# One set of rows per tile in the third stage: layer 2's scale and layer 3's statistics go back to rows together

## The chip, the cores and the metric

The kernel runs on one core of one Trainium2 chip. The metric is the device time of one execution in microseconds (us). The engines are named as in the profile: PE (TensorE; PEld is its loading of weights), DVE (VectorE), ACT (ScalarE), POOL (GpSimd) and SP (SyncE, which issues most transfers).

## The reference

The input x has 8192 samples of 8 channels of 16 x 16. Four layers follow each other, each of the form x = x + layer(gn(x)), where gn normalises each sample in 4 groups of 2 channels (mean and variance over 512 values). Layer 0 applies a tensor-train matrix and a bias. Layer 1 is a 3 x 3 convolution with batch normalisation and relu. Layers 2 and 3, the ones that matter here, are:

```python
# layer 2: quantised 3 x 3 convolution; sx comes from the largest |gn(x)| of all samples
sx = MAX_Q / jnp.max(jnp.abs(x));  sw = MAX_Q / jnp.max(jnp.abs(weight))
out_i32 = conv(_quantize(x, sx), _quantize(weight, sw))
out = out_i32 / (sx * sw) + bias
# layer 3: 3 x 3 convolution with edge padding, weights = sign times a mean of |w|
out = conv(pad(x, mode='edge'), binarize(weight)) + bias
```

In both, x inside the layer is gn(x); outside it is the running x.

## The kernel before, in words

The samples are cut into 64 tiles of 128 samples. A tile is [128 partitions, 2048 columns]: a partition is one channel and row of the image (c, h), a column is a sample and a w. A convolution is then three matmuls with banded 128 x 128 weights, one for each shift in w; 512 columns make one PSUM bank, two banks are half a tile.

There are three stages. The first does layer 0 and layer 1's convolution. The second adds layer 1 (its batch statistics are known by then), takes layer 2's statistics of every sample into `gnst`, subtracts the mean and finds the overall maximum. Then `sx` is formed, and the third stage does the rest of layer 2 and layer 3 for each tile. It takes tiles in `order`: first the 13 that stayed in SBUF, then the others, which are loaded from HBM four tiles ahead.

Statistics of a sample are made as columns with one sample per partition ([128, 4] for four groups), but are needed along the columns of a tile, the same for the 32 partitions of a group. The way back has two steps. `to_rows` multiplies each column by a mask into a diagonal tile `diag` on DVE (one product for each set of four columns) and transposes it in 32 x 32 blocks into `rows`. A matmul with a constant 0/1 selection matrix (`sel0`, `sel1`, `corr`) then spreads one set of columns over all partitions, into PSUM: `r2` (in `ps_a`) is layer 2's scale, `r3` (`ps_r`) layer 3's, `o3` (`ps_o`) layer 3's offset.

The operations of one tile i in the third stage, with engine and names as the profile shows them:

- `rows2` (DVE: diag_d, rows_d) and `spread2` (PE: ps_a<-rows_d): scale of layer 2.
- `scale2` "v" (DVE, two halves: v<-x,ps_a, to int8), `round2` "q" (ACT: q<-v, to bf16).
- `layer2` "c2h1", "c2h0" (PE: pq<-q,band, six matmuls for each half of the tile).
- `bias2` (ACT) adds the bias to half 0 of x; `first2` "stz" (DVE) adds half 0 of the product, pq x inv; `second2` "z1" (ACT: bs<-pq) writes half 1 into z3 and `add2` "add1" (POOL) adds it to x.
- `square3` "sq" (ACT), `sums3` "sums" (PE: s<-x,wsum and s<-sq,wsum, with 32 output columns each, four side by side in the array).
- `stats3` "small" (DVE: a reduction, a transposition into `st3`, then in `stats_small` a copy, a product and the variance into mv), `pow3` (POOL: mv to the power -1/2).
- `rows3` (DVE: mr = mean x scale, three diagonal products diag_e, transposition rows_e), `spread3` (PE: ps_r, ps_o<-rows_e), `offset3` "c" (ACT).
- `scale3` "t" (DVE, two halves), `high3` "hi" (ACT: rounds t, then the edge columns), `low3` "lo" (POOL: t - hi), `add3` "corr" (POOL: x + c), `edges3` "edl" (ACT: the edge columns of lo).
- `layer3` "c3h0a", "c3h0b", "c3h1a", "c3h1b" (PE: pf<-hi,sign and pf<-lo,sign; for each half of the tile six matmuls with hi and six with lo); `finish` "out0", "out1" (DVE: x<-pf,scale,x); after the second of them SP writes the tile out.

Tiles overlap as in a modulo schedule. Each operation has a time in `PHASE`; all operations of all tiles are sorted by PERIOD x i + PHASE (last lines of `tile_net`) and are issued in that order, through `InOrder`, which keeps each engine's program order. The times are sort keys alone: what runs when is decided on the chip by each engine's queue and the semaphores. Since `InOrder.__getattr__` issues nearly all operations, the profile gives L43 for them, and one goes by the names of tiles. PSUM is full: two slots of two banks for pq and pf together (`ps_c`), and a bank each for ps_a, ps_r, ps_o and s.

```python
todo = [(op, i) for _, op, i in sorted((PERIOD * i + at, op, i) for op, at in PHASE.items() for i in range(NT))]
for op, i in todo:
    if op == "rows2" and AHEAD <= i + 4 < NT:
        load3(i + 4)
    OPS[op](i)
```

Of the kernel before, what the change touches and what calls it, by code (L numbers as in the profile page):

```python
# [22 lines left out]
G = 4  # L23
# [9 lines left out]
class InOrder:  # L33
# [5 lines left out]
    def __getattr__(self, name):  # L39
        op = getattr(self.engine, name)  # L40

        def call(*args, **kwargs):
# [2 lines left out]

PERIOD = 11.539
PHASE = {"rows2": 0, "spread2": 0.01, "v": 5.1, "q": 10.2, "bias": 10.4, "c2h1": 11.6, "z1": 13.1, "c2h0": 16.1, "add1": 17.1,
         "stz": 23.1, "sq": 24, "sums": 31.8, "small": 34.7, "pow": 37.3, "rows3": 42.7, "spread3": 45.3, "t": 46.3,  # L50
         "hi": 49.9, "c": 51.2, "lo": 51.9, "corr": 58.8, "edl": 60.3, "c3h0a": 60.4, "c3h0b": 61.3, "out0": 66.8,
         "c3h1a": 69.3, "c3h1b": 69.4, "out1": 69.41}

PACK0 = [("c0", R * C), ("c1", R * H), ("core2", 2 * R * W), ("bias0", W)]
# [5 lines left out]
def tile_net(ctx: ExitStack, tc: tile.TileContext, xb, xt_in, pack0, pack1, pack2, out):  # L62
# [33 lines left out]
    T2 = [dict() for _ in range(NT)]  # L96

    LATE = 5 if NT >= KEEP + STAY + 3 else 0

    def load2(i, what="yx"):  # L100
        for k in what:
# [45 lines left out]
    def late_constants(late):  # L147
# [101 lines left out]
        quarter = L["quarter"] = blocks(32, 1.0, "quarter")  # L249
        gpad = L["gpad"] = const.tile([P, NQ, 32], F32, name="gpad")  # L250
        dve.memset(gpad, 0.0)
        dve.tensor_copy(gpad[:, :, 0:G], quarter.unsqueeze(1).to_broadcast([P, NQ, G]))
        for k, name in enumerate(("sel0", "sel1", "corr")):

            t = L[name] = const.tile([P, CH], F32, name=name)
            dve.tensor_copy(t.rearrange("p (g n) -> p g n", g=G),
                            mod32[:, G * k:G * k + G].unsqueeze(2).to_broadcast([P, G, CH // G]))
        yield "statistics"

    def diagonal(n):  # L260
        ts = []
        for k in range(2):
            t = const.tile([P, NQ, 32], F32, name=f"diag_{n}_{k}")
            nc.gpsimd.memset(t, 0.0)
            ts.append(t)
        return ts
# [8 lines left out]
    def samples(t):  # L275
        return t.rearrange("p (b w) -> p b w", w=W)
# [422 lines left out]
    def put_quarter(ps):  # L699
        nc.vector.tensor_copy(ps[:, 0:NQ], L["quarter"])  # L700

    def stats_small(mv, st, ps, name):

        s = small.tile([P, 32], F32, name=f"s_{name}", tag="s")
        dve.tensor_reduce(s, samples(ps), AX.X, ALU.add)
        dve.transpose(st, s)
        sq = small.tile([P, G], F32, name=f"sq_{name}", tag="sqm")
        dve.tensor_copy(mv[:, 0:G], st[:, 0:G])
        dve.tensor_tensor(sq, st[:, 0:G], mv[:, 0:G], ALU.mult)
        dve.scalar_tensor_tensor(mv[:, G:2 * G], st[:, G:2 * G], EPS, sq, ALU.add, ALU.subtract)  # L710

    def stats_pow(mv):
        pool.tensor_tensor(mv[:, G:2 * G], mv[:, G:2 * G], mhalf[:, :G], ALU.pow)

# [17 lines left out]
    with tc.tile_pool(name="p2", bufs=2) as p2, tc.tile_pool(name="ps2", bufs=2, space=PSUM) as ps2:  # L732
# [14 lines left out]
                                L["mean3"].unsqueeze(2).to_broadcast([P, C, H]), ALU.mult)  # L747
        nc.vector.tensor_tensor(L["corr"], L["corr"], ksum, ALU.subtract)

        def sum2(i):  # L750
            x, y = T[i]["x"], T[i].pop("y")
            y_used[i] = y
            act.activation(y, y, AF.Relu, bias=bn_b, scale=bn_a)
            pool.tensor_tensor(x, x, y, ALU.add)
# [8 lines left out]

        def stats2(i):

            st, mv = psc[:, 32 + 32 * (i % 2):64 + 32 * (i % 2)], gnst[:, order2[i]]
            red = small.tile([P, 32], F32, name=f"s_c{i}", tag="s")
            dve.tensor_reduce(red, samples(T[i].pop("ps")), AX.X, ALU.add)
            dve.transpose(st, red)
            T[i]["sq"] = small.tile([P, G], F32, name=f"sq_c{i}", tag="sqm")  # L770
            act.copy(mv[:, 0:G], st[:, 0:G])
            act.activation(T[i]["sq"], st[:, 0:G], AF.Square)

        def sigma2(i):
            st, mv = psc[:, 32 + 32 * (i % 2):64 + 32 * (i % 2)], gnst[:, order2[i]]
            dve.scalar_tensor_tensor(mv[:, G:2 * G], st[:, G:2 * G], EPS, T[i].pop("sq"), ALU.add, ALU.subtract)
            stats_pow(mv)

        def spread2(i):
            T[i]["gb"] = ps = ps2.tile([P, BANK], F32, name=f"gb_{i}", tag="gb")  # L780
            rows = to_rows(diag[i % 2], mask2, [gnst[:, order2[i]]], f"c{i}")
            if i % 4 == 0:
                T[i]["gr"] = ps2.tile([P, 4, P], F32, name=f"gr_{i}", tag="gr")
                T[i]["top"] = p2.tile([P, 4, P], F32, name=f"top_{i}", tag="top")
            else:
                T[i]["gr"], T[i]["top"] = T[i - 1]["gr"], T[i - 1]["top"]
            for dst, sel in ((ps[:, 0:P], L["sel0"]), (T[i]["gr"][:, i % 4], L["sel1"])):
                pe.matmul(dst, sel, rows, start=True, stop=True)
# [26 lines left out]
        def on(i, f):  # L815
            if 0 <= i < NT:
                f(i)
# [10 lines left out]
        for i in range(NT + 4):  # L828
            if i == 1:
                on(free, load2)  # L830
            if i + AHEAD2 < NT - LATE:
                on(i + AHEAD2, lambda i: i <= free or load2(i))
            elif late:
                k, j = late.pop(0)
                T2[j][k] = y_used[i - 1]
                nc.sync.dma_start(T2[j][k], (x1_d if k == "x" else y_d)[order2[j]])
            on(i, sum2)
            on(i - 2, sums2)
            on(i - 3, spread2)
            on(i - 1, square2)  # L840
            on(i - 2, stats2)
            on(i - 3, centre2)
            on(i - 2, sigma2)
            on(i - 3, range2)
# [9 lines left out]
    nc.vector.tensor_tensor(inv, sx, L["sw"], ALU.mult)  # L854
    nc.vector.reciprocal(inv, inv)

    gv = gnst[:, :, G:2 * G]
    nc.vector.tensor_scalar(gv, gv, sx, None, ALU.mult)

    with ExitStack() as s:
        wk = s.enter_context(tc.tile_pool(name="wk3", bufs=2))
        ps_c = s.enter_context(tc.tile_pool(name="ps_c3", bufs=2, space=PSUM))
        ps_s = s.enter_context(tc.tile_pool(name="ps_s3", bufs=1, space=PSUM))
        order = [*kept, *(t for t in range(NT) if t not in kept)]

        sq3, t3, z3 = sqs[0], [sqs[1], xh], [y_stay[3][:, h * F // 2:(h + 1) * F // 2] for h in range(2)]
        T = [dict() for _ in range(NT)]  # L870
        AHEAD = min(NT, KEEP - 6)
        diag2, diag3 = diagonal("d"), diagonal("e")

        ps_a, ps_r, ps_o = (ps_s.tile([P, BANK], F32, name=f"ps_{n}", tag=n) for n in ("a", "r", "o"))
        r2, r3, o3 = ps_a[:, 0:P], ps_r[:, 0:P], ps_o[:, 0:P]
        put_quarter(ps_a[:, P:2 * P])
        mask, st3 = ps_a[:, P:P + NQ], ps_a[:, P + 32:P + 64]

        def load3(i):
            t = order[i]  # L880
# [6 lines left out]
        def halves(t):  # L887
            return t.rearrange("p (h n) -> p h n", h=2)

        def rows2(i):  # L890
            T[i]["rows2"] = to_rows(diag2[i % 2], mask, [gnst[:, order[i], G:2 * G]], f"d{i}")

        def rows3(i):
            mv = T[i].pop("mv")
            mr = small.tile([P, G], F32, name=f"mr_{i}", tag="mr")
            dve.tensor_tensor(mr, st3[:, 0:G], mv[:, G:2 * G], ALU.mult)
            T[i]["rows3"] = to_rows(diag3[i % 2], mask, [mr, mv[:, G:2 * G], gnst[:, order[i], 0:G]], f"e{i}")


        def spread2(i):  # L900
            pe.matmul(r2, L["sel0"], T[i].pop("rows2"), start=True, stop=True)

        def spread3(i):
            rows = T[i].pop("rows3")
            pe.matmul(r3, L["sel1"], rows, start=True, stop=True)
            pe.matmul(o3, L["corr"], rows, start=True, stop=True)

        def scale2(i):

# [9 lines left out]
            T[i]["q"] = q  # L919

        def bias2(i):
            x = halves(T[i]["x"])[:, 0]
            act.activation(x, x, AF.Identity, bias=L["bias2"], scale=1.0)

        def layer2(i, h):
# [8 lines left out]
        def first2(i):  # L934
            x = halves(T[i]["x"])[:, 0]
            dve.scalar_tensor_tensor(x, T[i].pop(("pq", 0)), inv, x, ALU.mult, ALU.add)

        def second2(i):
            act.activation(z3[i % 2], T[i].pop(("pq", 1)), AF.Identity, bias=L["bias2"], scale=inv)

        def add2(i):
            x = halves(T[i]["x"])[:, 1]
            pool.tensor_tensor(x, x, z3[i % 2], ALU.add)

        def square3(i):
            act.activation(sq3, T[i]["x"], AF.Square)
# [3 lines left out]
            sums_pe(T[i]["ps"], T[i]["x"], sq3)  # L950

        def stats3(i):
            T[i]["mv"] = small.tile([P, 2 * G], F32, name=f"mv3_{i}", tag="mv")
            stats_small(T[i]["mv"], st3, T[i].pop("ps"), f"d{i}")

        def pow3(i):
            stats_pow(T[i]["mv"])

        def offset3(i):
            T[i]["c"] = small.tile([P, P], F32, name=f"c_{i}", tag="c")  # L960
# [41 lines left out]
        def finish(i, h):  # L1002
# [4 lines left out]
            if T[i]["done"] == 2:  # L1007
                nc.sync.dma_start(out[order[i]], T[i]["x"])
                T[i].clear()

        OPS = {"rows2": rows2, "spread2": spread2, "v": scale2, "q": round2, "bias": bias2,
               "c2h0": lambda i: layer2(i, 0), "stz": first2, "c2h1": lambda i: layer2(i, 1), "z1": second2, "add1": add2,
               "sq": square3, "sums": sums3, "small": stats3, "pow": pow3, "rows3": rows3, "spread3": spread3, "c": offset3,
               "t": scale3, "hi": high3, "lo": low3, "corr": add3, "edl": edges3,
               "c3h0a": lambda i: layer3(i, 0, 0), "c3h0b": lambda i: layer3(i, 0, 1), "out0": lambda i: finish(i, 0),
               "c3h1a": lambda i: layer3(i, 1, 0), "c3h1b": lambda i: layer3(i, 1, 1), "out1": lambda i: finish(i, 1)}
        todo = [(op, i) for _, op, i in sorted((PERIOD * i + at, op, i) for op, at in PHASE.items() for i in range(NT))]
        for i in range(AHEAD):
            load3(i)
        for op, i in todo:  # L1020
            if op == "rows2" and AHEAD <= i + 4 < NT:
                load3(i + 4)
            OPS[op](i)

# [68 lines left out]
```

## Time and profile before

| what | value |
| --- | --- |
| time, median of 3 runs (lowest to highest) | 3823.38 us (3821.75 to 3823.41) |
| profiled execution, its own time | 3824.58 us |
| its span | 3822.8 us |
| first stage | to about 2630 us |
| second stage | to about 3064 us |
| third stage | 3064 us to the end |
| mean granted clock of TensorE | 0.96 |
| busy over the span | PE 94%, DVE 89%, ACT 66%, POOL 80% |
| third stage, 3150 to 3250 us | PE 99.5, DVE 91.7, ACT 80.1, POOL 100.0 of 100 us |
| third stage, 3450 to 3550 us | PE 99.6, DVE 91.7, ACT 80.3, POOL 98.4 of 100 us |

The span is the time from the first to the last instruction of the profiled execution. A matmul's end is modelled and matmuls are pipelined, so PE's busy share says less than the distances between the starts of its instructions. The waits of an engine are inferred from semaphores: the last releaser by the profile is named, even where the engine could not have gone on without it either.

### The profile page before, as it was taken

How to read it: one execution, taken by the hardware profiler on the slowest of the kernel's cores; microseconds unless marked ns; L12 is line 12 of the kernel's file. 1: busy time of each engine (PE TensorE's matmuls, PEld its weight loads, DVE VectorE, ACT ScalarE, POOL GpSimd, SP SyncE). 2: the span in 40 equal slices, each digit the busy share in tenths (PEclk: the TensorE clock that was granted, in tenths of full speed). 3: DMA queues.
4: the chain of work that ended last, by engine and by line, in shares of the span. 5: the costliest groups of instructions: out<-in, count | busy, mean ns of one | idle time of the engine just before them, and what ended most of it. 6: DMA issues, size and time to landing. Idle time of an engine off the chain costs nothing.

```text
span 3822.8 us, 52777 instructions
## 1 busy us (share of the span) xinstructions
PE 3598.8 (94%) x16264; PEld 2127.1 (56%) x16326; DVE 3386.0 (89%) x6313; ACT 2518.2 (66%) x2676; POOL 3048.8 (80%) x3104
## 2 busy tenths in 40 slices
PE   8999999999999999999999999997665589999999
PEld 4666666666666666666666666663221145555555
DVE  8988888888888888888888888877998889999997
ACT  5666666666666666666666666665665578778775
POOL 4877777778777777787777777865887779999998
PEclk9999999999999999999999999998776689999999
DMA  5787787878877878878788878766999724444442
GB/s 212 254 270 256 258 269 252 265 258 258 271 253 261 272 253 262 262 250 272 254 263 270 257 258 265 253 200 253 419 424 424 326 90 186 182 183 187 181 161 110
DMA packets 210809, 960.93 MB, mean 251 GB/s; under 512 B 44896, under 2 KB 45152, under 8 KB 110048
## 3 DMA queue, kind: packets, MB, share of 16 engines
q1 hardware_dynamic: 173808, 692.22, 48.8%
q0 software_dynamic: 36288, 264.26, 23.5%
q8 instruction: 131, 2.15, 0.2%
q14 instruction: 150, 1.23, 0.1%
q10 hardware_dynamic: 432, 1.08, 0.1%
HBM read 578.84 MB, written 378.54 MB: 250 GB/s over the span
## 4 chain that ended last, share of the span: by engine, by line
PE 85%; DVE 6%; DMA 4%; issue 2%; POOL 1%; ACT 1%; POOLq 0%; SPq 0%; DVEq 0%; ACTq 0%
PE po L43 45%; PE pu L43 12%; PE pf L43 10%; PE pm L43 6%; PE pq L43 4%; PE s L43 3%; PE pc L43 3%; DVE top L43 3%; PE ps_r L43 1%; DMA ys<-x_d 1%; DMA x_d<-u 1%; DMA x_d<-ys 1%; DMA u<-x_d 1%; DMA x_d<-xs 1%; DMA sq<-y_d 1%
## 5 line engine op out<-in xcount | busy, mean ns | idle before, releaser
L43 PE MATMUL po<-u,core 128*128 128x512 f32 (+1 forms) x4112 | 1844.7, 591 | 0.0
L43 ACT COPY u<-pu 128x2048 f32<-128x2048 f32 x512 | 955.4, 1866 | 512.9 <-PE pu L43 512.8
L43 PEld LDWEIGHTS po<-u,core 128*128 128x128 f32 x4112 | 744.6, 190 | 737.0 <-issue 736.1
L43 PE MATMUL pu<-core2r,xl 128*128 128x256 f32 x4032 | 678.6, 310 | 4.5 <-ACT u L43 3.5
L43 PEld LDWEIGHTS pu<-core2r,xl 128*128 128x128 f32 x4032 | 527.9, 189 | 127.9 <-issue 123.1
L43 POOL TENSOR_TENSOR bs<-bs,xh 128x512 fp32r<-128x512 f32 (+1 forms) x253 | 325.1, 1285 | 203.0 <-ACT xh L43 203.0
L43 POOL TENSOR_TENSOR v<-e 128x128 f32<-128x128 f32 x750 | 396.7, 540 | 0.0
L43 DVE TENSOR_TENSOR xs<-po,xs 128x512 f32<-128x512 f32 x256 | 176.9, 691 | 218.8 <-PE po L43 218.6
L43 ACT ACTIVATE m<-pm,b 128x128 f32<-128x128 f32 x250 | 91.7, 367 | 395.3 <-PE pm L43 395.3
L43 PEld LDWEIGHTS pm<-v,fast 128*128 128x128 f32 x2000 | 262.5, 192 | 119.7 <-issue 105.7
L43 POOL TENSOR_TENSOR e<-x1n,x 128x512 f32<-128x512 f32 x250 | 305.9, 1223 | 23.2 <-ACT x L43 15.8
L43 DVE TENSOR_TENSOR bs<-bs,stat 128x1024 f32<-128x1024 f32 x252 | 290.6, 1215 | 2.1
L43 POOL TENSOR_TENSOR xs<-xs,w 128x2048 f32<-128x2048 f32 x64 | 291.4, 4552 | 0.6 <-DMA xs<-in_xt 0.6
L43 PE MATMUL pm<-v,fast 128*128 128x128 f32 x2000 | 263.6, 275 | 0.0
L43 ACT ACTIVATE x<-x1n 128x512 f32<-128x512 f32 x500 | 247.0, 545 | 7.6 <-DVE x1n L43 7.6
L43 POOL TENSOR_TENSOR mv<-mv,mhalf 128x4 f32<-128x4 f32 x127 | 130.8, 1030 | 135.9 <-DVE mv L43 135.9
L43 PE MATMUL pf<-hi,sign 128*128 128x512 f32 x768 | 231.1, 439 | 0.0
L43 POOL DMA_DIRECT2D xl<-limb_d x252 | 149.8, 594 | 101.3 <-ACT x L43 38.4
L43 PE MATMUL pf<-lo,sign 128*128 128x512 f32 x768 | 218.0, 422 | 0.3 <-ACT lo L43 0.3
L43 POOL TENSOR_TENSOR v<-r 128x128 f32<-128x128 f32 x500 | 215.2, 447 | 0.0
L43 ACT ACTIVATE sq<-xs 128x2048 f32<-128x2048 f32 x103 | 197.0, 1913 | 18.2 <-DVE xs L43 13.6
L43 PE MATMUL gb<-rows_c,sel 128*128 128x128 f32 x128 | 40.8, 413 | 166.3 <-DVE rows_c L43 166.3
(308 smaller groups left out, 7195.3 us busy)
## 6 DMA issues: line engine op xcount, KB each, us to landing
xl<-limb_d POOLq DMA_DIRECT2D x252, 1024.0 KB, 7.4
x_d<-xs SPq DMA_DIRECT2D x76, 1024.0 KB, 8.4
xs<-in_xt SPq DMA_DIRECT2D x64, 1024.0 KB, 7.6
bs<-in_xb SPq DMA_DIRECT2D x63, 1024.0 KB, 5.6
limb_d<-xh SPq DMA_DIRECT2D x1008, 64.0 KB, 4.4
limb_d<-bs SPq DMA_DIRECT2D x1008, 64.0 KB, 5.2
y_d<-ys SPq DMA_DIRECT2D x60, 1024.0 KB, 8.0
u<-x_d SPq DMA_DIRECT2D x34, 1024.0 KB, 6.5
```

The lines of the kernel that those rows point to most:

```text
L43: return self.tc.keep_in_program_order(op(*args, **kwargs))
```

## The change

Layer 2's scale and layer 3's three columns of statistics of a tile now sit side by side in one tile `cols`, four sets of four columns for each tile: mean x scale, scale, layer 2's mean, and layer 2's scale of the tile four further on (LEAD = 4). `rows2` and `spread2` are gone. One operation "rows" multiplies all 16 columns by the mask in one product, transposes once, and one operation "spread" does the three matmuls: `back2` (layer 2's scale of tile i+4), `sel1` and `corr` (layer 3 of tile i). For the first four tiles "rows" and "spread" run with i from -4 to -1, for back2 alone. `cols` is set to zero by GpSimd between the stages, and filled by DVE (layer 2's scales times sx, in place of the former product in gnst) and ACT (layer 2's means); gnst is kept in the order of use (`place`). `back2` is written in stage 2 over a weight that is no longer used.

Of layer 3's small statistics the copy and the square on DVE become one square on ACT ("sqm"), and the variance is an operation of its own ("var"), written straight into cols.

Of half 1 of layer 2's sum, SHARE = 16 of 64 samples (256 of 1024 columns) are added by DVE straight from PSUM ("stz1", `third2`), and ACT's `second2` and GpSimd's `add2` do the other 768. `bias2` covers these 256 columns too.

All times of PHASE are new, and so is the order that they make: on PE, in one round of the steady state, it was pf (two pairs), pq, sums, rows, pq; it becomes pf (two pairs), pq, rows, sums, pq. The load of tile i+4 goes with "v" of tile i.

```diff
-PERIOD = 11.539
-PHASE = {"rows2": 0, "spread2": 0.01, "v": 5.1, "q": 10.2, "bias": 10.4, "c2h1": 11.6, "z1": 13.1, "c2h0": 16.1, "add1": 17.1,
-         "stz": 23.1, "sq": 24, "sums": 31.8, "small": 34.7, "pow": 37.3, "rows3": 42.7, "spread3": 45.3, "t": 46.3,
-         "hi": 49.9, "c": 51.2, "lo": 51.9, "corr": 58.8, "edl": 60.3, "c3h0a": 60.4, "c3h0b": 61.3, "out0": 66.8,
-         "c3h1a": 69.3, "c3h1b": 69.4, "out1": 69.41}
+PERIOD = 11.25
+PHASE = {"v": 0, "q": 6.4, "c2h1": 13.9, "bias": 14.8, "c2h0": 16.4, "stz1": 16.9, "z1": 17.4, "stz": 20.7, "add1": 21.7,
+         "sq": 22.1, "sums": 27.1, "small": 29.9, "sqm": 30.6, "var": 32, "pow": 35.3, "rows": 36.7, "spread": 36.9,
+         "c": 37.6, "t": 39.6, "hi": 43, "lo": 49.1, "corr": 50.7, "edl": 52.2, "c3h1a": 58, "c3h1b": 58.5, "out1": 61.1,
+         "c3h0a": 64.8, "c3h0b": 67.2, "out0": 67.5}
+LEAD = 4
+SHARE = 16
...
+        def operands3():
+            L["select"]("back2", [3], L["band3"][:, 0])
...
+            if i == 8:
+                operands3()
...
-    gv = gnst[:, :, G:2 * G]
-    nc.vector.tensor_scalar(gv, gv, sx, None, ALU.mult)
...
+        cols = wk.tile([P, NT + LEAD, 4 * G], F32, name="cols", bufs=1)
+        nc.gpsimd.memset(cols, 0.0)
+        nc.vector.tensor_scalar(cols[:, 0:NT, 3 * G:4 * G], gnst[:, :, G:2 * G], sx, None, ALU.mult)
+        nc.scalar.copy(cols[:, LEAD:, 2 * G:3 * G], gnst[:, :, 0:G])
...
-        def rows2(i):
-            T[i]["rows2"] = to_rows(diag2[i % 2], mask, [gnst[:, order[i], G:2 * G]], f"d{i}")
+        def column(i, k):
+            return cols[:, i + LEAD, k * G:(k + 1) * G]
 
         def rows3(i):
-            mv = T[i].pop("mv")
-            mr = small.tile([P, G], F32, name=f"mr_{i}", tag="mr")
-            dve.tensor_tensor(mr, st3[:, 0:G], mv[:, G:2 * G], ALU.mult)
-            T[i]["rows3"] = to_rows(diag3[i % 2], mask, [mr, mv[:, G:2 * G], gnst[:, order[i], 0:G]], f"e{i}")
-
-
-        def spread2(i):
-            pe.matmul(r2, L["sel0"], T[i].pop("rows2"), start=True, stop=True)
+            if i >= 0:
+                dve.tensor_tensor(column(i, 0), st3[:, 0:G], column(i, 1), ALU.mult)
+            diag = diag3[i % 2]
+            dve.tensor_tensor(diag[:, :, 0:4 * G], cols[:, i + LEAD].unsqueeze(1).to_broadcast([P, NQ, 4 * G]),
+                              mask.unsqueeze(2).to_broadcast([P, NQ, 4 * G]), ALU.mult)
+            T3[i] = rows = small.tile([P, P], F32, name=f"rows_{i}", tag="rows")
+            dve.transpose(rows, diag.rearrange("p q j -> p (q j)"))
 
         def spread3(i):
-            rows = T[i].pop("rows3")
-            pe.matmul(r3, L["sel1"], rows, start=True, stop=True)
-            pe.matmul(o3, L["corr"], rows, start=True, stop=True)
+            rows = T3.pop(i)
+            for k, (dst, sel) in enumerate(((r2, "back2"), (r3, "sel1"), (o3, "corr"))):
+                if (i >= 0 if k else i + LEAD < NT):
+                    pe.matmul(dst, L[sel], rows, start=True, stop=True)
...
         def bias2(i):
-            x = halves(T[i]["x"])[:, 0]
+            x = T[i]["x"][:, 0:F // 2 + SHARE * W]
             act.activation(x, x, AF.Identity, bias=L["bias2"], scale=1.0)
...
+        def third2(i):
+            x = halves(T[i]["x"])[:, 1][:, 0:SHARE * W]
+            dve.scalar_tensor_tensor(x, T[i]["pq", 1][:, 0:SHARE * W], inv, x, ALU.mult, ALU.add)
+
         def second2(i):
-            act.activation(z3[i % 2], T[i].pop(("pq", 1)), AF.Identity, bias=L["bias2"], scale=inv)
+            act.activation(z3[i % 2][:, SHARE * W:], T[i].pop(("pq", 1))[:, SHARE * W:], AF.Identity, bias=L["bias2"], scale=inv)
 
         def add2(i):
-            x = halves(T[i]["x"])[:, 1]
-            pool.tensor_tensor(x, x, z3[i % 2], ALU.add)
+            x = halves(T[i]["x"])[:, 1][:, SHARE * W:]
+            pool.tensor_tensor(x, x, z3[i % 2][:, SHARE * W:], ALU.add)
...
         def stats3(i):
-            T[i]["mv"] = small.tile([P, 2 * G], F32, name=f"mv3_{i}", tag="mv")
-            stats_small(T[i]["mv"], st3, T[i].pop("ps"), f"d{i}")
+            red = small.tile([P, 32], F32, name=f"s_{i}", tag="s")
+            dve.tensor_reduce(red, samples(T[i].pop("ps")), AX.X, ALU.add)
+            dve.transpose(st3, red)
+
+        def square_mean3(i):
+            T[i]["sqm"] = small.tile([P, G], F32, name=f"sqm_{i}", tag="sqm")
+            act.activation(T[i]["sqm"], st3[:, 0:G], AF.Square)
+
+        def variance3(i):
+            dve.scalar_tensor_tensor(column(i, 1), st3[:, G:2 * G], EPS, T[i].pop("sqm"), ALU.add, ALU.subtract)
 
         def pow3(i):
-            stats_pow(T[i]["mv"])
+            pool.tensor_tensor(column(i, 1), column(i, 1), mhalf[:, :G], ALU.pow)
...
-            if op == "rows2" and AHEAD <= i + 4 < NT:
+            if op == "v" and AHEAD <= i + 4 < NT:
                 load3(i + 4)
```

## The prediction

> **What bounds the kernel now.** I read the page first: on the whole span PE is busy 94%, DVE 89%, POOL 80%. The change touches the third stage alone, so next came the table of stretches for that stage. Its columns are the stretch, its length, each engine's busy time with its count of instructions, the granted clock, the DMA share and GB/s:
>
> ```profile
> 3350.00:3450.00 100.00, 99.53 (x494) 59.08 (x505) 91.86 (x165) 79.61 (x71) 98.57 (x36) 1.00 0.49 189
> ```
>
> PE 99.5%, DVE 91.9%, ACT 79.6%, POOL 98.6%. PE or POOL: the shares don't say which. The chain of waits in order of time does (start, length, what):
>
> ```profile
> 3395.94 6.15 PE pf L43 x24
> 3402.09 0.66 PE pq L43 x3
> 3402.75 0.05 issue
> 3402.80 0.60 PE pq L43 x2
> 3403.40 1.85 PE s L43 x16
> 3405.25 0.42 PE ps_r L43 x2
> 3405.67 0.22 PE ps_o L43 x2
> 3405.89 0.22 PE ps_a L43 x2
> 3406.12 1.30 PE pq L43 x6
> 3407.41 6.15 PE pf L43 x24
> ```
>
> One tile takes 11.47 us (3395.94 to 3407.41), and every piece is PE. Whether PE itself waits in it shows in the timeline (start, length, instruction, idle time before). First the round at 3403, then an early one in which PE had nothing to hurry for:
>
> ```profile
> 3404.21 1.04 PE L43 MATMUL s<-sq,wsum 128*32 128x512 f32 x8
> 3404.66 0.31 DVE L43 STREAM_TRANSPOSE rows_d<-diag_d 128x128 f32<-128x128 f32 x1
> 3405.18 0.30 PEld L43 LDWEIGHTS ps_r<-rows_e,sel 128*128 128x128 f32 x2 [0.84 <-DVE rows_d L43]
> ...
> 3079.54 0.31 DVE L43 STREAM_TRANSPOSE rows_d<-diag_d 128x128 f32<-128x128 f32 x1
> 3080.31 1.04 PE L43 MATMUL s<-sq,wsum 128*32 128x512 f32 x8
> 3081.28 0.30 PEld L43 LDWEIGHTS ps_a<-rows_d,sel 128*128 128x128 f32 x2 [0.84 <-DVE xk L43]
> ```
>
> The list of waits charges 29.3 us in 35 tiles (0.84 each) to DVE's rows. But from the squares' sums to that weight load it is 0.97 us in both rounds, and in the early one the rows were done at 3079.85, 1.4 us before. So 0.97 us is PE's own time for leaving the 32-column sums, not a wait. **PE's instruction stream is the bound**; POOL follows it closely: lo 4.23 + corr 3.65 + pow 0.99 + add 2.41 (starts to starts) = 11.28, and it idles 0.18 for hi.
>
> PE's round from the starts of these blocks: 24 pf 6.15; 12 pq 2.60; sums 4 groups at 0.43 (3403.78 to 3404.21) = 1.72; rows 6 at 0.11 (3405.40, .62, .84 for the pairs) = 0.66; entering the sums 0.10 (pq to s takes 1.40 for 1.30); leaving them 0.13 (1.85 for 1.72) and 0.11 for a row weight load with nothing to hide behind (0.77 for 0.66). Sum 11.47.
>
> **What the Trainium skill says.** "TensorE: Matmul & The Clock Gate", "Architectural detail": PE's queue can pull weight loads ahead of running matmuls, while ACT and DVE take their queues strictly in order. Its "The mechanism" under "Part 3: Packing small matmuls" adds that a load overlaps with running matmuls only when it goes to other rows of the array. [...] "GPSIMD Engine Reference", section 3.1: about 2.6 cycles per element for an addition of two tensors, near twice DVE's; here 2.42 us against DVE's 1.21 for 1024 columns. "PSUM — Partial Sum Buffer", "PSUM bank collisions raise a hardware error": two engines must not read one bank together; this explains why in the new program second2 waits for third2, which reads the same pq. The trace of before has no such pair.
>
> **The change part by part**, per round of the steady state; names are those of the operations.
>
> POOL: add1 has 768 columns instead of 1024: 2.41 x 3/4 = 1.81, saves 0.60. POOL then has 10.68 us of work. PE's 11.47 hides the saving, so it is worth nothing by itself; were PE below 11.28, it would count in full.
>
> DVE: the mv copy and product go (0.20 + 0.19), three diagonal products and a separate fourth with its transposition become one product of 64 columns (saves 0.43 for rows2 and 0.17 - 0.05 = 0.12 in rows3); third2 comes in, 256 of 1024 columns of a 1.16 us operation, 0.08 + 0.27 = 0.35. Net -0.59, hidden too: DVE idles 0.62 per tile for pf.
>
> ACT: bias2 +256 and second2 -256 columns cancel (about 0.19 each way); one square of 4 columns, 0.17 at most by the same operation in stage 2 (sq_c). ACT is 79.6% busy; 0.17 hides there. If ACT were late by over 1.2 us, hi would hold the next c back (below).
>
> PE: the same matmuls in another order. Before, from pf: pq, sums, rows, pq, pf. After: pq, rows, sums, pq, pf. Entering the sums costs 0.10 either way. Leaving them now goes to pq: 0.13, plus a weight load of 0.10 (the length of a bf16 load) that can't hide either. So 11.46: **no gain on PE**. Nothing shows sums followed by pq; from below the bare load could be 0 (round 11.36), from above 0.11. I take 0.10, because the drain of the array before the switch is the same and only the type of the next weights differs.
>
> **The new wait.** Before, DVE waited for one pf pair, and from that pair's end PE had the other pair (3.07), pq (1.40) and the sums (1.85) to do, 6.32 us, before it wanted rows; DVE's way there (3398.85, when PE left the pair, to 3404.97, the transposition's end, + 0.05) took 6.17. Now rows stand in front of the sums, so PE wants them 1.85 us and more earlier. In the built program DVE's queue runs: out0 of tile n-6, v of n (two halves), mr, diagonal, transposition of n-3, out1. PE's runs: second pf pair of n-6 (h0), then pf pair h1 of n-5, pq, and rows of n-3. out0 needs the h0 pair finished, and v and rows are queued behind it. From the moment E at which PE leaves the h0 pair:
>
> - DVE: out0 starts E + 0.20 (PE started the next pair at 3410.33, DVE started out at 3410.53); out0 1.20 (to v at 3411.73); v 2.26 (3400.26 to mr at 3402.52); mr 0.19; diagonal 0.19 + 48 more columns at 1.1 ns = 0.24; transposition 0.31; 0.05 until PE loads (3799.22 + 0.31 to 3799.58, a round where PE did wait). Sum 4.45.
> - PE: pf pair 3.07, pq 1.30: it reaches the rows at E + 4.37, and would begin their weight load 0.11 ahead, at 4.26.
>
> Rows come 0.19 us late. PE is in order, so the sums, pq h0, both pf pairs and thus the next out0 all slip: a closed loop. Round 11.46 + 0.19 = 11.65, against 11.47: **+0.18**. SP's queue gets the load of tile i+4 at v of tile i instead of rows2 of i, still four rounds (46 us) before use against 7.6 us to landing, so the load stays hidden; the write out follows the second out as before.
>
> Other loops have slack. mr waits for POOL's pow of n-3, whose var stands at the end of the round before: done about E, needed at E + 3.66. hi of n-3 needs the buffer that h0 of n-5 reads: it starts after that half pair, then hi 1.96, edges 0.45, square 1.82, bias 1.24 = 5.47, and c's turn comes after 1.54 + 3.07 + 1.30 + 0.77 = 6.68: 1.2 us to spare. pf h0 needs third2 and second2 read out: about 1.6 us to spare.
>
> The ends. The memset of cols stands in POOL's queue in front of the all-reduce of the maximum, and waits for DVE's last use of the former memory (amax, ends 3063.45). 1088 columns, from 0.20 us for 128 and under 1 ns a column further, about 1.0 us: the all-reduce starts near 3064.5 instead of 3063.78: +0.7. Filling and draining do the same work in another order: I take +1.0, bounds -2 and +4. The third part for back2 is one DVE copy in stage 2, about 0.2 us, inside its share.
>
> Steady rounds: some 58 (3103.6 to 3780.4 is 59 rounds now). 58 x 0.18 = 10.4; + 0.7 + 1.0 = 12.1. The profiled execution took 3824.58 (span 3822.8, 1.8 around it), 1.2 over the median 3823.38; that is inside the spread of the runs shown. 3823.4 + 12.1 = 3835.5; 3824.6 + 12.1 = 3836.7. I say 3836.
>
> **The rivals.**
> 1. No change: leaving the sums towards pq costs only the 0.13, so the round is 11.36 + 0.19 = 11.55: 58 x 0.08 + 1.7 = +6 us, 3830; or DVE is 0.1 quicker than the sum, too: 3824. For it: no trace shows that switch. Against: the bare load after the sums is seen in every round. Chance 0.20.
> 2. Faster: the 0.84 us are a wait for data after all, POOL at 98.6% sets the round, and with rows ahead of the sums the 0.13 + 0.11 vanish. Round 11.47 - 0.24 = 11.23: -14 + 1.7, so 3811. It decides if DVE delivers rows by E + 4.26, that is 0.19 sooner than summed. For: the list of waits names DVE; against: the same 0.97 us in a round with rows long ready. Chance 0.10.
> 3. Much slower: ACT falls behind, because second2 stands behind third2 and q, edl, sqm and hi behind second2; past the 1.2 us of slack each 0.1 us adds 6 us: with 0.4 beyond it 3860. Against: ACT has 2 us idle per round. Chance 0.04.
>
> **How the numbers follow.** The late rows have the remaining 0.66 with 3829 to 3845: lateness 0.1 to 0.3 and the ends. A measurement of this kernel can tell about 0.2%, 7.6 us. Above 3831 counts as slower: most of the main case, rival 3, a little of rival 1: 0.69. Within: the rest of these, 0.21. Faster 0.10. For 8 in 10, rival 1 is taken in and rival 2 left out: 3823 to 3846.
>
> **What would show it.** PE's round 11.6 to 11.7 in the chain of waits, with DVE's rows in it between pq and ps_a, a gap of 0.1 to 0.3 before the rows' weight load, DVE idle over 1 us for pf, POOL near 92%. The gap from sums to pq: about 0.66 for the last group's 0.43. The prediction is wrong if the rows' weight load starts before the last pq ends, if rounds stay at 11.4, or if ACT or POOL enters the chain.

## The result, and the profile after

| | before | after |
| --- | --- | --- |
| time, median of 5 runs (lowest to highest) | 3823.41 us (3821.75 to 3825.23) | 3840.1 us (3839.12 to 3841.58) |
| ratio to before, 95% interval | | 1.0043 (1.0028 to 1.0058) |
| profiled execution, its span | 3822.8 us | 3838.0 us |

The kernel became slower by 16.7 us in the medians and by 15.2 us in the two spans. The forecast was 3836 us, slower. The total is close; two of its terms, the rounds and the start, are not, and their errors nearly cancelled.

The span's 15.2 us can be placed by marks that both traces have. All are starts, in us: the end of the second stage is the end of DVE's `pm` (the maximum over a partition); "first diag" is the first diagonal product of the third stage; the rounds are counted between the matmuls that bring the rows of tiles 3 and 59 back (in both kernels the matmul ps_r).

| stretch | before | after | difference |
| --- | --- | --- | --- |
| span's start to the first diag | 3065.04 | 3071.66 | +6.6 |
| first diag to the rows of tile 3 (filling) | 53.32 | 54.89 | +1.6 |
| rows of tile 3 to those of tile 59 (56 rounds) | 642.50 | 647.76 | +5.3 |
| rows of tile 59 to the end (draining) | 61.95 | 63.72 | +1.8 |

One round is 642.50 / 56 = 11.473 us before and 647.76 / 56 = 11.567 after.

**The steady state.** The table of stretches of the changed kernel, with the columns of the same table in the prediction (stretch, length, then busy time and instructions of PE, PEld, DVE, ACT and POOL, clock, DMA share, GB/s):

```profile
3350.00:3450.00 100.00, 100.00 (x495) 58.87 (x494) 85.95 (x123) 79.96 (x79) 92.39 (x36) 1.00 0.48 182
```

POOL went from 98.6% to 92.4% and DVE from 91.9% to 86.0%; PE now shows 100.0%. The relief is there, and the round is longer. A busier PE is not a better used PE here: ends of matmuls are modelled, and in the timeline the pq ahead of the rows is drawn to 3403.91 (3402.44 + 1.47), past the start of the rows' late matmul at 3403.84, so that this wait leaves no idle time. The chain of waits of the changed kernel shows it (start, length, what):

```profile
3402.60 1.31 PE pq L43 x6
3403.91 0.42 PE ps_a L43 x2
3404.33 0.22 PE ps_r L43 x2
3404.55 0.22 PE ps_o L43 x2
3404.77 1.85 PE s L43 x16
3406.63 1.40 PE pq L43 x6
3408.03 6.13 PE pf L43 x24
3414.16 1.31 PE pq L43 x6
```

The order is the new one, pq, rows, sums, pq, pf. Of three row pairs the first takes 0.42 and the others 0.22: 0.20 stands at the head of the rows. The timeline of the changed kernel says what it waits for (start, length, instruction, idle time before it and its releaser):

```profile
3399.37 1.70 PE L43 MATMUL pf<-hi,sign 128*128 128x512 f32 x6
3399.57 1.28 DVE L43 SCALAR_TENSOR_TENSOR u<-pf,scale,u 128x1024 f32<-128x1024 f32 x1 [1.46 <-PE pf L43]
3400.77 2.34 DVE L43 TENSOR_TENSOR v<-ys,ps_a 128x1024 int8<-128x1024 f32 x2
...
3403.03 0.15 DVE L43 TENSOR_TENSOR cols<-ps_a,cols 128x4 f32<-128x4 f32 x1
3403.22 0.22 DVE L43 TENSOR_TENSOR diag_d<-cols,ps_a 128x64 f32<-128x64 f32 x1
3403.47 0.31 DVE L43 STREAM_TRANSPOSE rows<-diag_d 128x128 f32<-128x128 f32 x1
3403.84 0.30 PEld L43 LDWEIGHTS ps_a<-rows,band 128*128 128x128 f32 x2 [0.42 <-DVE rows L43]
...
3405.59 1.04 PE L43 MATMUL s<-sq,wsum 128*32 128x512 f32 x8
3406.56 0.98 PEld L43 LDWEIGHTS <-band 128*128 128x128 bf16 x6 [0.84 <-issue]
3406.56 1.47 PE L43 MATMUL pq<-q,band 128*128 128x512 bf16 x6
```

Read from the top: PE leaves the h0 pair of pf at 3399.37 and starts the other pair; DVE has idled 1.46 us for that, then runs out0 ("u<-pf"), v, the column mean x scale, the product of 64 columns, the transposition. The rows' weight load starts at 3403.84, 4.47 us after PE left the pair. That is the closed loop of the prediction, with DVE in the middle of it. The last three lines are the squares' sums and what follows them: the weight load for pq shows 0.84 us of idle time, as a row load after the sums did before, and here it is put down to nothing but "issue".

**The start of the third stage.** The same view where the overall maximum is formed. Before:

```profile
3063.48 0.17 DVE L850 TENSOR_REDUCE pm<-amax 128x1 f32<-128x16 f32 x1
3063.78 0.38 POOL L851 PARTITION_ALL_REDUCE gm<-pm  x1 [8.52 <-DVE pm L850]
```

After:

```profile
3063.35 0.17 DVE L860 TENSOR_REDUCE pm<-amax 128x1 f32<-128x16 f32 x1
3063.51 1.00 POOL L874 MEMSET cols<- 128x1088 f32 x1 [8.37 <-DVE pm L860]
3064.55 0.40 ACT L876 COPY cols<-gnst 128x256 f32<-128x256 f32 x1 [12.37 <-POOL cols L874]
3070.17 0.38 POOL L861 PARTITION_ALL_REDUCE gm<-pm  x1 [5.65 <-issue]
```

The memset takes the forecast 1.00 us, and it is over by then: ACT's copy into cols, which waits for it, starts at 3064.55. But the all-reduce, which line 861 issues, comes 5.65 us after the memset's end, with no wait to blame. In the kernel before it came 0.14 us after the end of `pm`. What lies between shows if one asks for all instructions of that one line, those of the queue included (line, engine, operation, count, lowest/median/highest ns, first and last start). Before:

```profile
L851 POOLq MODIFY_POOL_CONFIG  x2: 12/12/12, 3055.2 to 3055.3; - x2
...
```

After:

```profile
L861 POOLq MODIFY_POOL_CONFIG  x2: 11/11/11, 3064.5 to 3064.5; - x2
...
```

Two instructions of POOL's queue come ahead of the all-reduce; by their name they change POOL's configuration. Before, they went out at 3055.2, as soon as the last pow of the second stage was done, while POOL idled 8.5 us for `pm`; whatever they start was over by then. Now the memset stands ahead of them in POOL's queue and waits for DVE (the profile names `pm`), so they go out at 3064.5, and the all-reduce pays for them. "GPSIMD Engine Reference" of the Trainium skill, section 2.1 "Instruction dispatch", says that this instruction can bring new code into the engine's memory, and that the first call of what was newly loaded pays about 6 us more (it gives 5.95 us as measured), with no instruction to be seen in the profile. The trace agrees in kind and nearly in size: 5.65 us here. That the code load itself fills these 5.65 us is the page's account; the runs below show where they come and go.

### The profile page after: what moved, and what is told of

The parts are those of the page before. It is cut to its first block, busy times and chain, and to the rows that moved or that the text cites. A ratio compares the mean times of both kernels' runs of the same rounds, so it can differ in the third digit from the quotient of the medians.

```text
span 3838.0 us, 52480 instructions
## 1 busy us (share of the span) xinstructions
PE 3610.6 (94%) x16326; PEld 2128.5 (55%) x16326; DVE 3356.6 (87%) x6002; ACT 2524.3 (66%) x2741; POOL 3014.4 (79%) x3103
## 4 chain that ended last, share of the span: by engine, by line
PE 87%; DVE 8%; DMA 2%; issue 2%; POOL 1%; ACT 0%; SPq 0%; DVEq 0%; POOLq 0%
PE po L43 45%; PE pu L43 12%; PE pf L43 10%; PE pm L43 6%; PE pq L43 4%; DVE top L43 3%; PE s L43 3%; PE pc L43 3%; DMA u<-x_d 1%; PE ps_a L43 1%; DVE xs L43 1%; PE gb L43 1%; DVE u L43 1%; DMA x_d<-xs 1%; POOL xs L43 1%
## 5 line engine op out<-in xcount | busy, mean ns | idle before, releaser
L43 POOL TENSOR_TENSOR mvb<-mvb,mhalf 128x4 f32<-128x4 f32 x64 | 66.3, 1036 | 167.5 <-DVE mvb L43 167.5
```

The costliest lines, as they stand in the source:

```text
L43: return self.tc.keep_in_program_order(op(*args, **kwargs))
```

## The experiments

Two theories were put to the test. The first: the start is late by the change of POOL's configuration, which the memset uncovers. The second: the rounds are longer because the rows come late through the loop of out0, v and the transposition, on a PE that by itself would be faster than before. The rivals: the memset's own length or the new small steps at the start; other engines, or a PE that by itself is no faster, for the rounds. The ratios are against the kernel before, 3823.94 us (39 runs) for the first four and 3823.79 us (15 runs) for the others. The sections below give this table's readings their reasons; all lengths are in us, the first column counting from the end of `pm`.

| kernel | all-reduce starts | filling | one round | draining | time |
| --- | --- | --- | --- | --- | --- |
| before | 0.14 | 53.32 | 11.473 | 61.95 | 3823.4 |
| after | 6.65 | 54.89 | 11.567 | 63.72 | 3840.1 |
| 1, memset on DVE | 0.14 | 52.91 | 11.567 | 63.57 | 3834.5 |
| 2, before with the memset | 6.52 | 52.36 | 11.473 | 61.98 | 3830.7 |
| 3, v before out0 | 6.60 | 54.42 | 11.410 | 63.59 | 3831.6 |
| 4, both mended | 0.14 | 55.65 | 11.410 | 63.83 | 3824.5 |
| 5, no share | 6.74 | 56.38 | 11.582 | 63.53 | 3841.2 |
| 6, both mended, no share | 0.14 | 54.48 | 11.410 | 63.52 | 3824.0 |
| 7, rows later | 6.53 | 58.15 | 11.926 | 63.94 | 3865.1 |
| 8, rows after the sums | 6.98 | 55.03 | 11.843 | 63.66 | 3854.6 |

From the first diag on, "before" and 2 do the same work, and so do "after" and 1; yet their fillings differ by 0.96 and 1.98 us. So much that stretch moves without a change in it; each trace is a single execution, and that of 1 was the fastest of its eight, 3.2 us under their median. The draining is steady: 61.95 and 61.98 in the old order, 63.5 to 63.9 in the new. But how the ends divide depends on the mark, for in the new order the rows stand ahead of the sums, which are 1.85 us of PE's round. Counted from the first matmul of the sums of tiles 3 and 59 instead of the rows', filling is 39.93 before and 43.86 after, and draining 75.28 and 74.74: +3.9 and -0.5, the same 3.4 together. So a longer draining is not shown; counted so, what the ends cost lies in the filling (39.93 and 39.03 in "before" and 2; 41.89 to 46.75 in "after", 1 and 3 to 7).

### 1. The memset of cols on DVE

```diff
-        nc.gpsimd.memset(cols, 0.0)
+        nc.vector.memset(cols, 0.0)
```

> The changed kernel with the zeroing of cols on DVE instead of GpSimd. Theory 1 (the zeroing holds GpSimd's change of library, 5.66 us, behind DVE's last maximum): the all-reduce starts within 0.5 us of pm again, the third stage starts 6.0 to 6.6 us earlier, 3833.5 to 3834.5 us. Rival (only the 1.0 us of the zeroing itself counts, the rest of the 6.4 us is another wait): 3839 us.

Measured: 3834.51 us (3831.29 to 3835.92, 8 runs), ratio 1.0028 (1.0018 to 1.0038): 5.6 us less than the changed kernel. Timeline of this kernel:

```profile
3063.39 0.38 POOL L861 PARTITION_ALL_REDUCE gm<-pm  x1 [8.51 <-DVE pm L860]
3063.64 0.96 DVE L874 MEMSET cols<- 128x1088 f32 x1 [0.39 <-issue]
```

The same memset takes 0.96 us on DVE, beside the all-reduce, which is back at 0.14 after `pm`. The first diag comes 0.67 later than before instead of 6.75. The memory is cleared as before; only POOL's queue is free, and its two configuration instructions go out at 3054.8, 8.6 us ahead of the all-reduce. So the 6 us hang on what stands in that queue. The round stays at 11.567.

### 2. The kernel before, with the memset

In the kernel before, at the same place of the third stage (nothing reads cols):

```diff
+        cols = wk.tile([P, NT + 4, 4 * G], F32, name="cols", bufs=1)
+        nc.gpsimd.memset(cols, 0.0)
```

> The kernel before with one thing of the change alone: a tile of the size of cols is allocated at the start of stage 3 and zeroed on GpSimd (nothing reads it). Theory 1: GpSimd's all-reduce starts 6.4 us later, 3829.5 to 3830.0 us, rounds stay at 11.47. Rival (the zeroing's own 1.0 us): 3824.4 us.

Measured: 3830.72 us (3829.36 to 3832.78, 14 runs), ratio 1.0018 (1.0010 to 1.0026): 6.8 us more than the kernel before, with the rounds at their 11.473. Timeline of this kernel, and the configuration instructions of line 851:

```profile
3063.28 1.00 POOL L866 MEMSET cols<- 128x1088 f32 x1 [8.37 <-DVE pm L850]
3069.81 0.38 POOL L851 PARTITION_ALL_REDUCE gm<-pm  x1 [5.52 <-issue]
...
L851 POOLq MODIFY_POOL_CONFIG  x2: 11/11/11, 3064.2 to 3064.3; - x2
```

The all-reduce waits 5.52 us of "issue" after the memset. One instruction of 1.00 us, added to a kernel in a place where its engine has nothing to do for 8.4 us, costs 6.8.

### 3. v ahead of out0 in DVE's queue

```diff
-PHASE = {"v": 0, "q": 6.4, ...
+PHASE = {"v": -0.1, "q": 6.4, ...
```

This puts v of tile n ahead of out0 of tile n-6 in the order of issue, so that v and the rows behind it no longer wait for PE's pf pair.

> The changed kernel with v of tile n ahead of out0 of tile n-6 in DVE's queue (its time in PHASE from 0 to -0.1), so that rows have 2.26 us less in front of them after the h0 pair. Theory 2 (rows come late by the loop h0 pair, out0, v, rows): PE no longer waits for rows, the round falls from 11.57 to about 11.37 us, 58 rounds give -11.5: 3828 to 3829.5 us. Rival (the 0.2 us between pq and the second row matmul is PE's own, as at the switch to the sums): round 11.57, 3840 us.

Measured: 3831.63 us (3829.53 to 3833.03, 14 runs), ratio 1.0020 (1.0012 to 1.0028): 8.5 us less than the changed kernel, where 11.5 were expected. The round is 11.410 (56 rounds in 638.96), not 11.37. The 0.20 at the rows' head is gone. What kept the rest is seen best in the next kernel, which has the same steady state.

### 4. Both mended

v as in 3, and only the columns that nothing else writes are cleared, on DVE:

```diff
-PHASE = {"v": 0, "q": 6.4, ...
+PHASE = {"v": -0.1, "q": 6.4, ...
...
-        nc.gpsimd.memset(cols, 0.0)
+        nc.vector.memset(cols[:, 0:LEAD, 0:3 * G], 0.0)
+        nc.vector.memset(cols[:, NT:, 3 * G:], 0.0)
```

> The changed kernel with v ahead of out0 and with only the parts of cols that nothing else writes zeroed, on DVE. Theories 1 and 2 together: 3840.1 - 6.5 - 11.5 = 3822 us (3820.5 to 3823.5), a round of 11.37 us against 11.47 before, but some 3 us more at the start and in the last rounds. If either falls, 3829 or 3834 us.

Measured: 3824.45 us (3822.94 to 3826.59, 13 runs), ratio 1.0002 (0.9994 to 1.0010): the kernel before, within what can be measured, though above the 3820.5 to 3823.5 us expected. With both causes taken away the loss is gone. Its chain of waits over one round:

```profile
3408.24 6.15 PE pf L43 x24
3414.39 0.66 PE pq L43 x3
3415.05 0.05 issue
3415.10 0.59 PE pq L43 x2
3415.70 0.22 PE ps_a L43 x2
3415.92 0.22 PE ps_r L43 x2
3416.14 0.22 PE ps_o L43 x2
3416.37 1.85 PE s L43 x16
3418.22 1.40 PE pq L43 x6
3419.62 6.20 PE pf L43 x24
```

All three row pairs now take 0.22: nothing is late, and PE's own round is 3419.62 - 3408.24 = 11.38. Set beside the round before: there, sums 1.85, rows 0.42 + 0.22 + 0.22 and pq 1.30, together 4.01; here 0.66, 1.85 and 1.40, together 3.91. Behind the sums a row pair costs 0.20 extra and the pq 0.10 extra (the chain counts by ends; by starts it is 0.11 and 0.01), and that 0.1 is all that the new order saves. The next pf block takes 6.20 instead of 6.15, and so in turn: rounds of 11.38 and 11.44, mean 11.410. In the blocks of 6.20 the last 18 of the 24 matmuls stand slightly further apart, 0.259 us instead of 0.2555; what for was not settled.

Against the kernel before this one gains 642.50 - 638.96 = 3.5 us in the rounds and pays 2.3 in filling and 1.9 in draining, 4.2 together by the marks of the table. Its first diag comes 1.39 after the end of `pm`, as before.

### 5. No share of the residual sum for DVE

In the changed kernel:

```diff
-SHARE = 16
+SHARE = 0
...
-         ... "c2h0": 16.4, "stz1": 16.9, "z1": 17.4, ...
+         ... "c2h0": 16.4, "z1": 17.4, ...
...
-   ... "stz1": third2, "z1": second2,
+   ... "z1": second2,
```

> The changed kernel with SHARE = 0: DVE's part of half 1 of the sum is undone, GpSimd adds all 1024 columns. Theory: GpSimd has 11.28 us of work in a round of 11.57 us and DVE's 0.35 us lie behind its rows, so nothing changes: round 11.57, 3839.5 to 3841 us. Rival (GpSimd's relief is worth its 0.6 us, or a part): round 11.7 or more, 3848 us and up. Or DVE's 0.35 us matter: 3820 us.

Measured: 3841.24 us (3840.88 to 3841.84, 4 runs), ratio 1.0046 (1.0031 to 1.0061). POOL is back at 96.9% and the time is that of the changed kernel, 1.1 us above it, with a round of 11.582 for 11.567. In the changed kernel the share is worth next to nothing. The trace has the wider pf blocks of 4 in 22 of the 51 rounds between 3140 and 3740 us, where the changed kernel has none.

### 6. Both mended, no share

Kernel 4 with the edit of 5. Its PE wants a round of 11.41, and the prediction put POOL's work without the share at 11.28, so here the share has its best chance.

> The version with v ahead of out0 and the zeroing on DVE, with SHARE = 0. GpSimd has 11.28 us of work and waits about 0.1 to 0.2 us for hi, PE's own round is 11.37. Theory (PE is the bound, GpSimd just fits): 3822 us as with the share, at most 2 us more. Rival (GpSimd becomes the bound at 11.46, so the share is what the shorter round needs): 3827 to 3828 us.

Measured: 3823.96 us (3821.34 to 3826.48, 12 runs), ratio 1.0001 (0.9992 to 1.0009). Its table of stretches:

```profile
3350.00:3450.00 100.00, 99.53 (x493) 60.21 (x499) 86.58 (x116) 80.34 (x80) 98.84 (x36) 1.00 0.48 184
```

POOL at 98.8% and the round at 11.410, the same to the last digit as with the share. POOL just fits; it waits 0.17 us for hi in every other round. This also settles how the prediction's second rival was to be read: a POOL as full as before does not set the round.

### 7. The rows 0.3 us later

The transposition into rows issued twice:

```diff
-            dve.transpose(rows, diag.rearrange("p q j -> p (q j)"))
+            for _ in range(2):
+                dve.transpose(rows, diag.rearrange("p q j -> p (q j)"))
```

> The changed kernel with the transposition into rows issued twice, the second over the first, so that rows are 0.24 to 0.35 us later in each round. Theory 2: the lateness passes into the round in full, 11.80 to 11.92 us, 3854 to 3861 us. Rival (PE's own switch): there is slack of the hidden load, round 11.57 to 11.65, 3840 to 3845 us.

Measured: 3865.14 us (3862.95 to 3865.82, 4 runs), ratio 1.0107 (1.0092 to 1.0122). The round is 11.926, 0.36 longer, for a second transposition that takes 0.34 with its gap. The chain of waits of this kernel has the loop in the open:

```profile
3407.50 3.12 PE pf L43 x12
...
3410.64 1.28 DVE u L43
3411.93 2.26 DVE v L43 x2
3414.18 0.08 DVE cols L43
...
3414.54 0.32 DVE rows L43
...
3414.89 0.32 DVE rows L43
...
3415.26 0.49 PE ps_a L43 x2
```

From the pf pair the chain goes to DVE and comes back to PE at ps_a: here PE's other pair and pq are not in the chain at all. In the changed kernel the two ways were so close (0.2 apart) that the chain stayed on PE and showed the wait only as 0.42 for 0.22. What DVE takes longer, every round takes longer; DVE's idle time for pf (1.46 us a round in the changed kernel) is no help, because it lies ahead of out0. The filling grew too, by 3.3 us, which took the total slightly above what was expected.

### 8. The rows after the sums again

The changed kernel with the rows' matmuls behind the sums, as before the change:

```diff
-         ... "spread": 36.9,
-         "c": 37.6, ...
+         ... "spread": 38.4,
+         "c": 38.5, ...
```

> The changed kernel with PE's rows behind the sums again (spread's time in PHASE from 36.9 to 38.4, c's with it), DVE's order left as it is. Simple reading (rows' lateness is all that the order costs): round 11.47, 3834.5 us. Theory 2 read to the end (DVE's t stands right behind rows, out1 and stz1, and now waits for PE's sums before it; DVE gives up its idle time, and small, stz, var and the next out0 slip): round 11.6 to 11.75, 3842 to 3850 us.

Measured: 3854.55 us (3853.69 to 3855.50, 4 runs), ratio 1.0080 (1.0063 to 1.0097), round 11.843. Neither reading was right; this is slower than both. The timeline of the weight loads of this kernel, with DVE's transposition:

```profile
3408.04 0.31 DVE L43 STREAM_TRANSPOSE rows<-diag_d 128x128 f32<-128x128 f32 x1
...
3410.30 0.30 PEld L43 LDWEIGHTS ps_a<-rows,band 128*128 128x128 f32 x2 [0.84 <-DVE ys L43]
...
3412.58 1.06 PEld L43 LDWEIGHTS pf<-hi,sign 128*128 128x128 f32 x5 [0.54 <-ACT bs L43]
```

Two things are in it. The rows were done at 3408.35, and their weight load after the sums still shows 0.84, now charged to another DVE instruction: 0.84 is what PE takes to leave the sums, in a steady round too. And pf waits for second2 (ACT bs). In the timeline of ACT, offset3 "c" stands ahead of second2 and had waited 2.83 us for ps_o; c began at 3411.28, second2 at 3411.55, and it took 0.98. So the rows that come late hold c, c holds second2, and second2 holds the PSUM that pf writes. Here are the two lines of ACT:

```profile
3411.28 0.37 ACT L43 ACTIVATE c<-ps_o,bias 128x128 f32<-128x128 f32 x1 [2.83 <-PE ps_o L43]
3411.55 0.98 ACT L43 ACTIVATE bs<-pq,bias,inv 128x768 f32<-128x768 f32 x1
```

The pf block takes 6.47 and 0.04 for 6.15, 0.36 more, which is the difference between 11.843 and the 11.473 of before's order but for 0.01. About 0.06 of it (18 times 0.0035) is the wider spacing of the pf matmuls seen in 4, which all rounds have here; some 0.3 are left for the wait. The new queue of ACT is made for rows that come before the sums; the order on PE cannot be put back alone.

## Why the prediction came out as it did

**PE is the bound, POOL is not: right.** POOL at 92.4% (after) or 98.8% (6) changes no round by more than 0.02. The savings on POOL and DVE were costed at nothing, with PE's round as the work that hides them. 5 and 6 show that for POOL. DVE's 0.59 went into idle time: it waits 1.46 us a round ahead of out0, for 0.62 before.

**The 0.84 us are no wait for data: right.** Kernel 8 shows them with the rows 1.9 us early, and the changed kernel shows them in front of pq.

**The late rows: right, and nearly to size.** Summed: rows at 4.45 us after PE leaves the h0 pair; measured 4.47. The round came out at 11.567, just under the announced 11.6 to 11.7, for the reason given next. Forecast lateness 0.19 a round; measured 11.567 - 11.38 = 0.19, made of 0.09 (pq to ps_a takes 1.40 by starts, 1.31 with nothing late) and 0.10 for the first row pair, whose weight load comes late too (0.32 by starts, 0.22 with nothing late). Against the mended kernels' mean round of 11.410, which has the wider pf blocks in it, the difference is 0.16. Taking v out of the loop (3) removes it; making DVE's part longer (7) adds what it is made longer by.

**PE's own round of 11.46: wrong.** The step that failed is "plus a weight load of 0.10 (the length of a bf16 load) that can't hide either". From the squares' sums to the first pq it takes 0.97, the same as it took to the rows, and from that pq to pf 1.12 (3406.56 to 3407.68) against 1.11 before (3405.95 to 3407.06). The prediction's own sign for the step, 0.66 from the last group of the sums to pq, came out as 0.54 (0.97 - 0.43). The load that stands bare after the sums costs 0.01 when the matmuls behind it are pq's and 0.11 when they are the short row matmuls. So PE's own round is 11.38, or 11.44 with the wider pf block; this was the first rival's figure (11.36, and 11.55 with the late rows; measured 11.567). Forecast for the rounds was +10.4; it became 5.3 over the 56 rounds between the marks. The section "The mechanism" of the Trainium skill's "TensorE: Matmul & The Clock Gate", which the prediction cites for loads that overlap with matmuls only when they go to other rows of the array, doesn't fit these traces: the pf loads, which take all 128 rows, run beside the pf matmuls, which take all 128 as well (each six loads start 0.25 us ahead of their matmuls, 3399.12 and 3399.37 in the changed kernel, take 0.19 each, and the matmuls still follow each other at 0.2555). The same section names the background weight buffer as a second way to load ahead, which the prediction left out and these traces don't contradict.

**The start, +0.7: wrong by 5.9.** The memset was seen, placed and sized rightly (1.0 us, waiting for DVE's last use of the memory). The term left out the two queue instructions that belong to the all-reduce. They have no busy time, so no table of the page lists them; the instructions of line 851 of the kernel before, with those of the queue, show them at 3055.2, 8.6 us ahead of the all-reduce. The prediction followed what moves in SP's queue instruction by instruction, and costed POOL's queue by busy times alone. The price itself stood in the section of the Trainium skill named above.

**The ends, +1.0: measured +3.4**, inside the bounds of -2 and +4. By the marks of the rows it is 1.6 filling and 1.8 draining; by those of the sums 3.9 and -0.5. Counted so, the filling is longer in every kernel with the new order, also where PE does not wait in the rounds (4 and 6). Why stays open.

**ACT and the rivals.** ACT has its slack in the changed kernel: it does not appear in the chain of the rounds, though second2 waits 0.20 us a round for third2 there, as the prediction explains from "PSUM — Partial Sum Buffer" of the Trainium skill. In 8, where c was made late, ACT does hold pf. Rival 2 (faster) fell, as above. Rival 3 did not occur in the changed kernel; 8 shows its mechanism, second2 late for pf, at about 0.3 a round.

Forecast 10.4 + 0.7 + 1.0 = 12.1; measured 5.3 + 6.6 + 3.4 = 15.2 by the spans. The sign would have held with either error alone, but that the total came within 4 us is partly luck: the rounds were sized 5 us too high and the start 6 us too low.

Mended in both places, the kernel is as fast as before (4 and 6), not faster: 0.06 a round over 56 rounds is 3.5 us, and the ends (4.2 and 2.7 together) take it back or nearly. Nothing that was run points to a version clearly below both.

## What to carry to other kernels

Ask for a line's queue instructions before anything is put ahead of it: what has no busy time can still be followed by 5.5 to 6.0 us of nothing, hidden only as long as it is issued early. When a matmul is moved ahead of others, follow its operand back to the instruction of its own engine that released it; if that path is longer than what the engine does meanwhile, it is a closed loop, and idle time elsewhere on that path's engine doesn't shorten it. The bare cost of a switch between kinds of matmuls depends on what follows it, so take it from a row that has the same follower, or keep both ends.

## What was not expected of the hardware

- The change of POOL's configuration ahead of the all-reduce is followed by 5.5 to 6.0 us (5.65 after, 5.52 in 2, 5.98 in 8) in which POOL does nothing and no instruction shows.
- Leaving the 32-column sums costs 0.11 us more before 128-column fp32 matmuls than in an even flow of them, and 0.01 before bf16 matmuls of 512 columns; the profile shows 0.84 of idle weight loading in both, once with an engine's name and once as "issue".
- The same 24 pf matmuls take 6.15 or 6.20 us by turns in 3, 4 and 6, with the last 18 of them 0.259 instead of 0.2555 us apart. All rounds of 8 have the wider spacing, none of "before", "after", 1 and 2. Open.
- Weight loads of all 128 rows run beside matmuls that use all 128: pf loads of 0.19 us each in a flow of matmuls 0.2555 apart.
